# Pre-activation convolution with quantised weights: another mix of combined and plain images, later quotients on ScalarE, twelve image tiles

## The chip, the cores and the metric

The kernel runs on one core of one Trainium2 chip. A core has five engines with queues of their own: TensorE (matrix products, PE in the profile, its weight loads PEld), VectorE (DVE), ScalarE (ACT), GpSimd (POOL) and SyncE (SP), which here only issues transfers. The metric is the device time of one execution in microseconds; a profiled execution also gives a span, from the first to the last recorded instruction.

## What is computed

The input x has 160 images of 128 channels and 32 x 32 pixels. Each image is normalised in 32 groups of 4 channels, then convolved 3 x 3 with one of five sets of weights, and added to x. The weights are quantised in two steps from the range of the whole array U. Image i of the kernel's own order belongs to set n = i // 32.

```python
def conv(x, U):                       # N = 5 sets, K = 3, 128 channels
    s1 = (max(U) - min(U)) / 3.0
    v1 = s1 * floor(U / s1)
    s2 = s1 / 5.0
    v2 = s2 * floor((U - v1) / s2)
    w = (v1 + v2).reshape(128 * N, 128, 3, 3)
    xb = x.reshape(160 // N, N * 128, 32, 32)
    return conv_general_dilated(xb, w, padding=1, feature_group_count=N)

def gn(v, G=32, eps=1e-5):            # per image and group of 4 channels
    return (v - mean) / sqrt(var + eps)

out = x + conv(gn(x), U)
```

## The kernel before

The order of all work is written out by hand: `run` loops over the 160 images, and each engine gets its instructions in the order in which that loop emits them. Images are loaded in pairs into tiles of a pool `xpool` (11 tiles of two images), `LOAD_LEAD` = 18 images ahead. They are measured (sum and sum of squares, on ScalarE but for the eight images of `BY_VECTOR`) `STAT_LEAD` + 1 images ahead. Then the normalised image is split into a 16-bit high and a 16-bit low part, so that products of 16-bit numbers keep enough precision.

The convolution exists in two forms, chosen by `combined(i)`:

- A plain image has z (normalised, 32 bits; GpSimd at L668 or ScalarE at L594), `hi` (ScalarE, L602), `lo` (VectorE, L697) and three combinations of rows of lo (VectorE, L710, L718, L719, tile `rows`). On TensorE the high part goes through nine taps for even and odd rows (18 matmuls, `taps`), the low part through 12 products of combinations (`product`): 30 matmuls.
- A combined image has sums and differences of neighbouring columns of x in a tile `v` of 2048 numbers (GpSimd L632 and L662, VectorE L644 and L651), its high part `vh` (ScalarE, L684) and its low part `vl` (VectorE, L690). Both parts go through 12 products: 24 matmuls.

Before the change images from 7 to 125 are combined when odd, those from 126 (`FIFTHS`) to 145 three in five, and from 146 (`THIRDS`) two in three.

For each image `sums_of_pairs(i + 1)` leaves two partial results in PSUM, ScalarE copies one out (`leave`, L837), VectorE makes the sum and the difference of the two (`pairs`, L846 and L848) as the start of that image's output banks `eo`, and `main` adds the other products to them. The result is added to x in one of two ways (`residual`): ScalarE copies eo to a tile `sum` (L874) and GpSimd issues a transfer that adds it to the image's tile (`accumulate`, L897), or, for images of `by_hand`, VectorE adds it itself (L891). `store` writes a finished pair of images to memory from SP's queue, in which loads, stores and weight loads (`load_set`, L448) stand in one order.

The weights of set n + 1 are made while set n runs. `load_set` fetches them; `make_column` is a generator that makes one column of the 3 x 3 taps; each `take(later, 1)` in the loop emits its next VectorE instruction. The generator's core is `quantise`: a quotient rounded to the nearest integer (`nearest`, L101), five steps that turn it into a floor (L109 to L113), the remainder (L127), and the same again with the second step size. Then the columns are turned by TensorE (`turn_column`), copied to the weight table by ScalarE (L527) and summed by VectorE (`sums_of_set`). The first set is made at the start, where columns alternate between the engines: `over_partitions` brings the range of U to all partitions, `from_range` makes the step sizes, and `warm_up` fills gaps of TensorE with matmuls whose result isn't used.

Of the kernel before, what the change touches and what calls it, by code (L numbers as in the profile page):

```python
# [22 lines left out]
LAST = 4  # L23
# [6 lines left out]

WIDEST = 40.0


class Steps:
# [60 lines left out]

    def nearest(self, pool, v, parts, name, dt, by_scalar=False):

        tag = "m" if by_scalar else "nn"
        n = pool.tile(list(v.shape), dt, tag=tag, name=f"n{tag}_{name}")
        engine = self.nc.scalar.mul if by_scalar else self.nc.vector.tensor_scalar_mul  # L100
        return n, engine(n, v, parts[0])  # L101
# [12 lines left out]

    def quantise(self, pool, un, name, dt, by_scalar=False):


        ints = mybir.dt.int16 if dt == MM else I32
        nn, first = self.nearest(pool, un, self.parts1, name, ints, by_scalar)
# [10 lines left out]
        nn, first = self.nearest(pool, rest, self.parts2, name + "_2", ints)  # L130
        yield first
        yield from self.floor_div(k2, rest, nn, tt, below, self.parts2)
        return k1, k2
# [212 lines left out]
class Main:  # L346
# [24 lines left out]
    STAT_LEAD = 14  # L371
    LOAD_LEAD = 18
    STEADY = 7
    BY_VECTOR = (8, 10, 11, 14, 19, 24, 29, 34)
    FIFTHS = 126
    THIRDS = 146
# [9 lines left out]
    def __init__(self, tc, ctx, keep, x, u, out):  # L386
# [16 lines left out]
        self.upool = pool("u", 1)  # L403
        self.xpool = pool("x", 11)
        self.zpool = pool("z", 3)
        self.parts = pool("parts", 5)
        self.rows = pool("rows", 4)
# [71 lines left out]
    def over_partitions(self, ext1, ident, between):  # L479


        nc, P = self.nc, self.P

        place = self.bank_pair("range").rearrange("p h r w -> p h (r w)")
        rows = place[0:1, 0, : 2 * P].rearrange("p (k c) -> p k c", k=2)
        for k in range(2):
            nc.tensor.transpose(rows[:, k, :], ext1[:, k : k + 1], ident)
        between()
        top = self.const.tile([1, 2], F32, tag="top", name="top")
        nc.vector.tensor_reduce(top, rows, AX.X, ALU.max)  # L490
        spread = place[:, 1, :2]
        nc.tensor.matmul(spread, self.ones, top, start=True, stop=True)
        return spread

    def make_column(self, n, col, by_scalar=False):
# [92 lines left out]

    def normalise(self, i):
        nc = self.nc  # L590
        st = self.stats[self.group_of[i]]
        j = i - self.groups[self.group_of[i]].start
        z = self.zpool.tile([self.P, 1024], F32, tag="z", name=f"z{i}")
        nc.scalar.activation(  # L594
# [10 lines left out]
    def combined(self, i):  # L605
# [142 lines left out]

    def warm_up(self, count):


        zeros = self.los[3].rearrange("p h w -> p (h w)")
        for _ in range(count):
            self.nc.tensor.matmul(
                self.pair[0].rearrange("p i w -> p (i w)"), zeros[:, :128],
                zeros[:, :512], start=True, stop=True,
# [149 lines left out]
    def run(self):  # L906
# [38 lines left out]

        self.ones = self.const.tile([1, P], F32, tag="ones", name="ones")
        nc.vector.memset(self.ones, 1.0)
        ext1 = self.weight_range(list(self.us.values()))
# [16 lines left out]
        def parts(i):  # L965
# [69 lines left out]
        ready, middle, scaled, measured, loaded = [], [], [], self.EARLY, 6  # L1035
        later, turned = iter(()), []
        for i in range(self.imgs):
# [34 lines left out]
            to_measure = range(measured, min(self.imgs, ahead))  # L1072
            measured += len(to_measure)
            if n + 1 < N_SETS:
                if b == (2 if n == 0 else 0):
                    self.load_set(n + 1)
                if b == (4 if n == 0 else 2):
                    later = (s for col in self.COLS for s in self.make_column(n + 1, col))
            by_scalar = [k for k in to_measure if not self.by_vector(k)]
            by_vector = [k for k in to_measure if self.by_vector(k)]  # L1080

            if i < self.FIRST:

# [14 lines left out]
            else:  # L1098
# [8 lines left out]
                last = take(later, 1, last)  # L1107
                for st in scaled:
# [32 lines left out]
            for n_of, col in turned:  # L1141
                self.keep_taps(n_of, col)
                if col == self.COLS[-1]:
                    later = self.sums_of_set(n_of)
            turned = []

            if i >= self.FIRST:
# [5 lines left out]
                else:  # L1153
                    take(later, 1)
                if b == self.per_set - 4:
                    run(later)
                for st in ready:
# [65 lines left out]
```

## Time and profile before

| | us |
|---|---|
| median of 3 runs | 983.02 |
| the three runs | 983.02, 977.3, 989.84 |
| the profiled execution | 982.18 |
| its span | 980.5 |

The page of the profile gives each engine's busy time, share of the span and number of instructions, and the share of a chain of waits that is followed back from the last instruction. A row of a group has the line in the code, the engine, the operation, the tiles written and read with their shapes, how often it occurs, then its busy time in us and the mean of one in ns, then the idle time of the engine just before it and who ended that. A row of a stretch of time has, for each engine, the busy time and the number of instructions, then the clock granted to TensorE, the share of the 16 DMA engines and GB/s. An interval is read with care: successive instructions of one engine overlap a little, so sums of means are somewhat larger than the time they take together.

The transfers, from the page:

| transfer | count | KB each | median us to landing |
|---|---|---|---|
| load of a pair of images (SP) | 78 | 1024 | 7.0 |
| store of a pair (SP) | 78 | 1024 | 8.7 |
| adding a sum to an image (POOL) | 137 | 512 | 7.2 |
| weights of a set (SP) | 4 | 576 | 9.7 |

### The profile page before, as it was taken

The page shows a single profiled execution, that of the slowest core. Times are in us where ns is not written, and L with a number is a line of the kernel's source. Part 1 is how long each engine was busy: PE and PEld are TensorE (multiplying, and loading weights), DVE is VectorE, ACT ScalarE, POOL GpSimd, SP SyncE. Part 2 cuts the span into 40 slices and gives each one's busy share as a digit, 9 for nine tenths or more (in the row PEclk, how much of TensorE's full clock was granted, in tenths as well). Part 3 has the DMA queues.
Part 4 walks back from the last instruction along what each step waited for, and adds up shares of the span by engine and source line. Part 5 has one row for each costly group of instructions (what it writes and reads, how often), then busy time and mean ns, then how long its engine had stood idle before and what let it go on. Part 6 is the DMA issues. An engine that isn't in the chain of part 4 may idle for free.

```text
span 980.5 us, 13236 instructions
## 1 busy us (share of the span) xinstructions
PE 943.3 (96%) x4504; PEld 440.8 (45%) x4504; DVE 913.8 (93%) x1332; ACT 833.4 (85%) x1135; POOL 353.5 (36%) x441
## 2 busy tenths in 40 slices
PE   2899999999999999999999999999999999999997
PEld 1444444444444444444444444444444444444443
DVE  7999999998999999899999998799999998989995
ACT  5779889999999999889898989698989899898551
POOL 4353333343333333333343333233433434333530
PEclk9999999999999999999999999999999999999999
DMA  9627889999998888999998999998989989998774
GB/s 352 264 95 207 230 236 267 265 250 257 319 297 242 269 232 244 257 289 273 250 267 240 272 247 253 285 281 265 239 261 259 258 249 269 247 247 251 178 207 160
DMA packets 65117, 245.86 MB, mean 251 GB/s; under 512 B 5008, under 2 KB 5008, under 8 KB 65040
## 3 DMA queue, kind: packets, MB, share of 16 engines
q1 hardware_dynamic: 45312, 173.09, 49.4%
q0 software_dynamic: 19728, 71.84, 38.8%
q8 instruction: 37, 0.61, 0.2%
q14 instruction: 40, 0.33, 0.1%
HBM read 89.19 MB, written 83.89 MB: 177 GB/s over the span
## 4 chain that ended last, share of the span: by engine, by line
PE 74%; DVE 12%; DMA 6%; issue 4%; ACT 2%; POOL 2%; SPq 0%; DVEq 0%; POOLq 0%
PE eo L789 25%; PE eo L734 23%; PE m L789 12%; PE m1b L789 8%; PE m1a L789 5%; DMA out_dram<-xt 3%; DVE vl L690 2%; DVE v L644 1%; DMA u<-in_L_conv_U_dram 1%; DVE lo L697 1%; DVE eo L846 1%; DMA xt<-sum 1%; DMA range<-in_L_conv_U_dram 1%; DVE eo L848 1%; DVE v L651 1%
## 5 line engine op out<-in xcount | busy, mean ns | idle before, releaser
L734 PE MATMUL eo<-hi,wt 128*128 128x496 f16 (+2 forms) x1386 | 367.7, 375 | 0.7 <-ACT wt L527 0.7
L789 PEld LDWEIGHTS <-wt 128*128 128x128 f16 x1884 | 183.9, 99 | 216.1 <-DVE rows L719 5.2
L734 PEld LDWEIGHTS <-wt 128*128 128x128 f16 x1458 | 142.6, 99 | 163.7 <-ACT wt L527 1.4
L874 ACT COPY sum<-eo 128x1024 f32<-128x1024 f32 x137 | 143.1, 1045 | 63.2 <-PE eo L789 63.0
L690 DVE SCALAR_TENSOR_TENSOR vl<-v,rstd,vh 128x2048 f16<-128x2048 f32 x82 | 192.2, 2344 | 1.4 <-ACT vh L684 1.4
L789 PE MATMUL eo<-vh,wt 128*128 128x496 f16 (+1 forms) x492 | 185.0, 376 | 1.0 <-DVE eo L848 0.9
L789 PE MATMUL eo<-vl,wt 128*128 128x496 f16 (+1 forms) x492 | 184.9, 376 | 0.0
L684 ACT ACTIVATE vh<-v,rstd 128x2048 f16<-128x2048 f32 x82 | 164.1, 2001 | 17.1 <-DVE v L651 16.9
L209 ACT ACTIVATE junk<-xt,mv 128x1024 f16<-128x1024 f32 x152 | 174.3, 1147 | 0.1
L202 ACT ACTIVATE junk<-xt 128x1024 f16<-128x1024 f32 x152 | 160.6, 1057 | 15.2 <-DMA xt<-in_x_dram 11.6
L789 PE MATMUL eo<-rows,wt 128*128 128x496 f16 (+1 forms) x450 | 170.8, 380 | 0.0
L789 PEld LDWEIGHTS <-across 128*128 128x128 f16 x984 | 96.2, 98 | 116.0 <-issue 5.1
L668 POOL TENSOR_SCALAR z<-xt,ngm,rstd 128x1024 f32<-128x1024 f32 x53 | 62.8, 1184 | 232.3 <-DVE tt L109 39.6
L632 POOL TENSOR_SCALAR v<-xt,ngm 128x64 f32<-128x64 f32 x82 | 30.9, 377 | 257.1 <-issue 72.7
L897 POOL DMA_DIRECT2D xt<-sum x137 | 119.8, 878 | 4.4 <-ACT sum L874 3.1
L837 ACT ACTIVATE m<-m 128x512 f32<-128x512 f32 x157 | 94.0, 599 | 24.9 <-PE m L789 18.7
L644 DVE TENSOR_TENSOR v<-xt 128x960 f32<-128x960 f32 x82 | 106.2, 1295 | 2.8 <-POOL v L632 2.8
L789 PE MATMUL m<-vl,across 128*128 128x496 f16 (+1 forms) x246 | 92.1, 374 | 3.3 <-DVE vl L690 3.2
L697 DVE TENSOR_TENSOR lo<-z,hi 128x1024 f16<-128x1024 f32 x78 | 94.9, 1216 | 0.0
L789 PE MATMUL m<-vh,across 128*128 128x496 f16 (+1 forms) x246 | 92.1, 375 | 0.0
L662 POOL TENSOR_TENSOR v<-xt 128x512 f32<-128x512 f32 x82 | 84.8, 1034 | 0.0
L602 ACT CAST hi<-z 128x1024 f16<-128x1024 f32 x78 | 81.5, 1044 | 1.2 <-POOL z L668 0.5
(144 smaller groups left out, 1151.8 us busy)
## 6 DMA issues: line engine op xcount, KB each, us to landing
xt<-in_x_dram SPq DMA_DIRECT2D x78, 1024.0 KB, 7.0
out_dram<-xt SPq DMA_DIRECT2D x78, 1024.0 KB, 8.7
xt<-sum POOLq DMA_DIRECT2D x137, 512.0 KB, 7.2
u<-in_L_conv_U_dram SPq DMA_DIRECT2D x4, 576.0 KB, 9.7
xt<-in_x_dram SPq DMA_DIRECT2D x4, 512.0 KB, 9.9
range<-in_L_conv_U_dram SPq DMA_DIRECT2D x3, 576.0 KB, 8.1
out_dram<-xt SPq DMA_DIRECT2D x3, 512.0 KB, 2.7
u<-in_L_conv_U_dram SPq DMA_DIRECT2D x2, 288.0 KB, 3.0
```

What stands on the lines that cost most here:

```text
L202: self.nc.scalar.activation(junk, image, ACTF.Copy, scale=-1.0 / image.shape[1], accum_out=self.mv[:, j, 0:1],)
L209: self.nc.scalar.activation(junk, image, ACTF.Square, bias=self.mv[:, j, 0:1], accum_out=self.mv[:, j, 1:2],)
L644: nc.vector.tensor_tensor(self.view(v, 1, (511, 2), (half, H), (1, half - 1)), self.view(x, 1, (1, 2), (W, H), (2, half - 1)), self.view(x ...
L662: ins = nc.gpsimd.tensor_sub(self.v[i][:, 1536:], odd, even)
L684: self.nc.scalar.mul(vh, self.v[i], st.rstd[:, j])
L690: yield self.nc.vector.scalar_tensor_tensor(vl, self.v[i], st.rstd[:, j], self.hi[i], ALU.mult, ALU.subtract)
L697: self.nc.vector.tensor_sub(lo[:, 1 : self.H + 1, :].rearrange("p h w -> p (h w)"), self.z.pop(i), self.hi[i].rearrange("p h w -> p (h w)"),)
L734: nc.tensor.matmul(self.bank(target, a)[:, first:end, c0:c1], self.wts[n, col][:, k, :], tile[:, s0 : s0 + 2 * (end - first) - 1 : 2, c0 + ...
L789: self.nc.tensor.matmul(out, weights, moving, start=start and j == 0, stop=False, skip_group_check=True)
L837: self.nc.scalar.mul(m2, self.m2_ps, 0.5)
L874: nc.scalar.copy(self.as_banks(i, self.sum[i]), self.flat(i, eo))
L897: self.nc.gpsimd.dma_start(self.image(i), self.sum.pop(i), accum_op=ALU.add)
```

## The change

It has six parts. `combined` becomes: odd images up to 29, then three in five (i % 5 in 0, 2, 4) up to 145, then three in four. In the weights of sets 1 to 4, both rounded quotients of a column are made by ScalarE: the generator yields a mark `SCALAR` ahead of each, and a new class `Later` passes no further step until `take_scalar`, at the end of the turn, emits it. In the first set's second column ScalarE makes both quotients. `xpool` has 12 tiles and `LOAD_LEAD` is 20; `zpool` goes from 3 to 2, `parts` from 5 to 4, and the tile that takes ScalarE's unread output is uint8. Weights are fetched earlier (for sets 2 to 4 at turn b = 30, the last but one, of the set two before), their making starts one image earlier, and what is left of it is emitted at b = 28 and b = 30. `by_hand` names every sixteenth image where it named every eighth. At the beginning the range is brought to all partitions by two matmuls with a broadcast operand and one VectorE reduction, image 4 is prepared one turn later, and there are eleven more filling matmuls.

```diff
+class Later:
+    def __init__(self, steps=()):
+        self.steps = iter(steps)
+        self.scalar = False
+    def take(self, count, last=None):
+        for _ in range(count):
+            if not self.scalar:
+                step = next(self.steps, None)
+                self.scalar = step is SCALAR
+                last = last if self.scalar else step or last
+        return last
+    def take_scalar(self):
+        if self.scalar:
+            next(self.steps)
+            self.scalar = False
+    def finish(self):
+        run(self.steps)
...
-    def quantise(self, pool, un, name, dt, by_scalar=False):
+    def quantise(self, pool, un, name, dt, by_scalar=()):
...
+        if "later" in by_scalar:
+            yield SCALAR
+        nn, first = self.nearest(
+            pool, un, self.parts1, name, ints, 1 in by_scalar,
+            "m" if 1 in by_scalar and "later" not in by_scalar else "nn",
+        )
...
-    LOAD_LEAD = 18
+    LOAD_LEAD = 20
-    FIFTHS = 126
+    FIFTHS = 30
...
-        self.xpool = pool("x", 11)
-        self.zpool = pool("z", 3)
-        self.parts = pool("parts", 5)
+        self.xpool = pool("x", 12)
+        self.zpool = pool("z", 2)
+        self.parts = pool("parts", 4)
...
-        rows = place[0:1, 0, : 2 * P].rearrange("p (k c) -> p k c", k=2)
+        rows = place[:, 0, : 2 * P].rearrange("p (k c) -> p k c", k=2)
         for k in range(2):
-            nc.tensor.transpose(rows[:, k, :], ext1[:, k : k + 1], ident)
+            nc.tensor.matmul(
+                rows[:, k, :], ext1[:, k : k + 1].to_broadcast([P, P]), ident,
+                start=True, stop=True,
+            )
         between()
-        top = self.const.tile([1, 2], F32, tag="top", name="top")
-        nc.vector.tensor_reduce(top, rows, AX.X, ALU.max)
-        spread = place[:, 1, :2]
-        nc.tensor.matmul(spread, self.ones, top, start=True, stop=True)
+        spread = self.const.tile([P, 2], F32, tag="top", name="top")
+        nc.vector.tensor_reduce(spread, rows, AX.X, ALU.max)
         return spread
...
-            junk = self.unread.tile([self.P, 1024], MM, tag="junk", name=f"junk{i}_{s}")
+            junk = self.unread.tile([self.P, 1024], mybir.dt.uint8, tag="junk", name=f"junk{i}_{s}")
...
+        if i == self.FIRST - 1:
+            z = self.sums.tile([self.P, 1024], F32, tag="sum", name=f"z{i}")
...
-        return (i - self.FIFTHS) % 5 % 2 == 0 if i < self.THIRDS else i % 3 != 1
+        return i % 5 % 2 == 0 if i < self.THIRDS else i % 4 != 2
...
-        if i < self.FIRST or i >= self.imgs - LAST:
-            return True
-        return i > self.BY_VECTOR[-1] - 4 and i % 8 == 7
+        return i < self.FIRST or i >= self.imgs - LAST or i > self.FIFTHS and i % 16 == 7
...
-            self.make_column(0, col, by_scalar=col != self.COLS[0]) for col in self.COLS
+            self.make_column(0, col, by_scalar=which)
+            for col, which in zip(self.COLS, ((), (1, 2), (1,)))
...
         take(third, 1)
+        take(second, 1)
         measure(1, 4)
+        self.warm_up(9, self.m1b)
         run(second)
         self.keep_column(0, self.COLS[1])
+        self.warm_up(2, self.m1b)
...
+            if i == 2:
+                self.load_set(1)
+            if b == self.per_set - 2 and n + 2 < N_SETS:
+                self.load_set(n + 2)
             if n + 1 < N_SETS:
-                if b == (2 if n == 0 else 0):
-                    self.load_set(n + 1)
-                if b == (4 if n == 0 else 2):
-                    later = (s for col in self.COLS for s in self.make_column(n + 1, col))
+                if b == (4 if n == 0 else 1):
+                    later = Later(
+                        s for col in self.COLS for s in self.make_column(n + 1, col, (1, 2, "later"))
+                    )
...
                 if i == 0:
                     measure(0, 8, 9, 10)
+                if i == 1:
                     self.normalise(4)
                     self.high_part(4)
...
-                    take(later, 1)
+                    later.take(1)
+                later.take_scalar()
-                if b == self.per_set - 4:
-                    run(later)
+                if b in (self.per_set - 4, self.per_set - 2):
+                    later.finish()
```

More of the change, by code (lines that the diff above doesn't have):

```diff
@@ L31 @@
 WIDEST = 40.0
+SCALAR = "the next step is ScalarE's"
+class Later:
[15 more added lines that the diff above has]
+        run(self.steps)
 class Steps:
@@ L94, in choose, with nearest @@
         nc.vector.tensor_copy(self.far, far)
-    def nearest(self, pool, v, parts, name, dt, by_scalar=False):
-        tag = "m" if by_scalar else "nn"
+    def nearest(self, pool, v, parts, name, dt, by_scalar=False, tag="nn"):
         n = pool.tile(list(v.shape), dt, tag=tag, name=f"n{tag}_{name}")
@@ L113, in floor_div @@
         yield nc.vector.tensor_sub(k, n, below)
-    def quantise(self, pool, un, name, dt, by_scalar=False):
+    def quantise(self, pool, un, name, dt, by_scalar=()):
         ints = mybir.dt.int16 if dt == MM else I32
-        nn, first = self.nearest(pool, un, self.parts1, name, ints, by_scalar)
+        if "later" in by_scalar:
[4 more added lines that the diff above has]
+        )
         yield first
@@ L129, in quantise @@
         )
-        nn, first = self.nearest(pool, rest, self.parts2, name + "_2", ints)
+        if "later" in by_scalar:
+            yield SCALAR
+        nn, first = self.nearest(
+            pool, rest, self.parts2, name + "_2", ints, 2 in by_scalar
+        )
         yield first
@@ L484, in over_partitions, with make_column @@
         place = self.bank_pair("range").rearrange("p h r w -> p h (r w)")
-        rows = place[0:1, 0, : 2 * P].rearrange("p (k c) -> p k c", k=2)
+        rows = place[:, 0, : 2 * P].rearrange("p (k c) -> p k c", k=2)
         for k in range(2):
-            nc.tensor.transpose(rows[:, k, :], ext1[:, k : k + 1], ident)
+            nc.tensor.matmul(
+                rows[:, k, :], ext1[:, k : k + 1].to_broadcast([P, P]), ident,
+                start=True, stop=True,
+            )
         between()
-        top = self.const.tile([1, 2], F32, tag="top", name="top")
-        nc.vector.tensor_reduce(top, rows, AX.X, ALU.max)
-        spread = place[:, 1, :2]
-        nc.tensor.matmul(spread, self.ones, top, start=True, stop=True)
+        spread = self.const.tile([P, 2], F32, tag="top", name="top")
+        nc.vector.tensor_reduce(spread, rows, AX.X, ALU.max)
         return spread
-    def make_column(self, n, col, by_scalar=False):
+    def make_column(self, n, col, by_scalar=()):
         nc, P = self.nc, self.P
@@ L592, in normalise @@
         j = i - self.groups[self.group_of[i]].start
-        z = self.zpool.tile([self.P, 1024], F32, tag="z", name=f"z{i}")
+        if i == self.FIRST - 1:
+            z = self.sums.tile([self.P, 1024], F32, tag="sum", name=f"z{i}")
+        else:
+            z = self.zpool.tile([self.P, 1024], F32, tag="z", name=f"z{i}")
         nc.scalar.activation(
@@ L747, in bank, with warm_up @@
         return target[h] if target is self.pair else target[:, h]
-    def warm_up(self, count):
+    def warm_up(self, count, bank=None):
         zeros = self.los[3].rearrange("p h w -> p (h w)")
@@ L754, in warm_up @@
             self.nc.tensor.matmul(
-                self.pair[0].rearrange("p i w -> p (i w)"), zeros[:, :128],
+                (bank or self.pair[0]).rearrange("p i w -> p (i w)"), zeros[:, :128],
                 zeros[:, :512], start=True, stop=True,
@@ L944, in run @@
             self.los.append(lo)
-        self.ones = self.const.tile([1, P], F32, tag="ones", name="ones")
-        nc.vector.memset(self.ones, 1.0)
         ext1 = self.weight_range(list(self.us.values()))
@@ L1035, in run @@
         ready, middle, scaled, measured, loaded = [], [], [], self.EARLY, 6
-        later, turned = iter(()), []
+        later, turned = Later(), []
         for i in range(self.imgs):
@@ L1073, in run @@
             measured += len(to_measure)
+            if i == 2:
+                self.load_set(1)
+            if b == self.per_set - 2 and n + 2 < N_SETS:
+                self.load_set(n + 2)
             if n + 1 < N_SETS:
-                if b == (2 if n == 0 else 0):
-                    self.load_set(n + 1)
-                if b == (4 if n == 0 else 2):
-                    later = (s for col in self.COLS for s in self.make_column(n + 1, col))
+                if b == (4 if n == 0 else 1):
+                    later = Later(
+                        s for col in self.COLS for s in self.make_column(n + 1, col, (1, 2, "later"))
+                    )
             by_scalar = [k for k in to_measure if not self.by_vector(k)]
@@ L1104, in run @@
                     self.low_part(i + 2)
-                    take(later, 1)
+                    later.take(1)
                     last = last_of(self.combinations(i + 2))
-                last = take(later, 1, last)
+                last = later.take(1, last)
                 for st in scaled:
@@ L1143, in run @@
                 if col == self.COLS[-1]:
-                    later = self.sums_of_set(n_of)
+                    later = Later(self.sums_of_set(n_of))
             turned = []
@@ L1153, in run @@
                 else:
-                    take(later, 1)
-                if b == self.per_set - 4:
-                    run(later)
+                    later.take(1)
+                later.take_scalar()
+                if b in (self.per_set - 4, self.per_set - 2):
+                    later.finish()
                 for st in ready:
```

## The prediction

> **What bounds the kernel now.** I read the page's busy shares and the shares of its chain of waits first.
>
> ```profile
> PE 943.3 (96%) x4504; PEld 440.8 (45%) x4504; DVE 913.8 (93%) x1332; ACT 833.4 (85%) x1135; POOL 353.5 (36%) x441
> ...
> PE 74%; DVE 12%; DMA 6%; issue 4%; ACT 2%; POOL 2%; SPq 0%; DVEq 0%; POOLq 0%
> ```
>
> TensorE carries the chain, with VectorE close behind. Next, the busy times by stretch of the span (engines in the order PE, PEld, DVE, ACT, POOL; at the end the clock, the DMA share and GB/s).
>
> ```profile
> 175.00:200.00 25.00, 24.43 (x118) 11.31 (x117) 24.79 (x36) 23.45 (x32) 8.76 (x13) 1.00 0.93 263
> 300.00:350.00 50.00, 50.00 (x242) 23.45 (x241) 49.47 (x76) 44.72 (x63) 17.93 (x21) 1.00 0.86 246
> 600.00:650.00 50.00, 47.80 (x221) 21.59 (x220) 41.05 (x58) 41.80 (x58) 15.28 (x18) 0.97 0.93 268
> 800.00:850.00 50.00, 50.00 (x240) 23.31 (x238) 45.37 (x57) 46.52 (x64) 18.94 (x22) 1.00 0.97 266
> ```
>
> TensorE is full from 200 us on but for one stretch. VectorE is full (99%) where later weights are being made (300 to 350) and has a tenth free where they are not (800 to 850, already three combined images in five). Before 200 us it is VectorE that is full, and TensorE loses 4.3 us between 100 and 200 (95.7 us busy). Third, the groups by shape give prices.
>
> ```profile
> L690 DVE SCALAR_TENSOR_TENSOR vl<-v,rstd,vh 128x2048 f16<-128x2048 f32 x82 | 192.2, 2344 | 1.4 <-ACT vh L684 1.4
> L684 ACT ACTIVATE vh<-v,rstd 128x2048 f16<-128x2048 f32 x82 | 164.1, 2001 | 17.1 <-DVE v L651 16.9
> L644 DVE TENSOR_TENSOR v<-xt 128x960 f32<-128x960 f32 x82 | 106.2, 1295 | 2.8 <-POOL v L632 2.8
> L697 DVE TENSOR_TENSOR lo<-z,hi 128x1024 f16<-128x1024 f32 x78 | 94.9, 1216 | 0.0
> L602 ACT CAST hi<-z 128x1024 f16<-128x1024 f32 x78 | 81.5, 1044 | 1.2 <-POOL z L668 0.5
> L651 DVE SCALAR_TENSOR_TENSOR v<-xt,twice 128x512 f32<-128x512 f32 x82 | 60.7, 741 | 0.0
> L710 DVE TENSOR_TENSOR rows<-lo 128x1024 f16<-128x1024 f16 x75 | 51.3, 684 | 0.8
> L718 DVE TENSOR_TENSOR rows<-lo 128x512 f16<-128x512 f16 x75 | 31.1, 415 | 0.0
> L719 DVE TENSOR_TENSOR rows<-lo 128x512 f16<-128x512 f16 x75 | 31.1, 414 | 0.0
> L101 DVE TENSOR_SCALAR nnn<-u,s1r 128x384 int16<-128x384 f32 x13 | 6.2, 477 | 6.1 <-DMA u<-in_L_conv_U_dram 6.0
> L101 DVE TENSOR_SCALAR nnn<-rest,s2r 128x384 int16<-128x384 f32 x15 | 6.2, 414 | 0.0
> L101 ACT ACTIVATE nm<-u,s1r 128x384 int16<-128x384 f32 x2 | 1.6, 806 | 0.1
> ```
>
> A combined image costs VectorE 1295 + 741 + 2344 = 4380 ns, a plain one 1216 + 684 + 415 + 414 = 2729 ns; ScalarE 2001 against 1044. One wait stands out in VectorE's own list, and the timeline shows it:
>
> ```profile
> 614.19 0.46 SPq L448 DMA_DIRECT2D u<-in_L_conv_U_dram  x1
> ...
> 626.17 0.47 DVE L101 TENSOR_SCALAR nnn<-u,s1r 128x384 int16<-128x384 f32 x1 [5.95 <-DMA u<-in_L_conv_U_dram]
> ...
> 627.98 0.82 PE L789 MATMUL m<-rows,wt 128*128 128x512 f16 x3 [2.01 <-DVE rows L719]
> ```
>
> The weights' transfer was issued late and took 12 us; VectorE stood 5.95 us in front of its first step, the rows of the next image came late, TensorE stood 2.0 us and then ran some matmuls at 0.6 us. From the starts of the second combination (L848), images 29 to 61 take 185.2 us, 61 to 93 185.2, 93 to 125 (with this wait) 190.95: it cost 5.7 us.
>
> **What the skill says.** The page "TensorE: Matmul & The Clock Gate" (section "Wait — 56ns, not 53.3ns?") gives N/2.4 GHz plus 2.5 ns per warm matmul, an estimate of 1.268 us for one of 512 and two of 496 columns, twice; the chain shows 1.27 for six, so TensorE has no slack inside and only fewer matmuls help. "ScalarE: Activation LUTs" ("What ACT_TABLE_LOAD costs") gives 186 + 0.833 N ns plus 93 for a pointer operand: 599 ns for N = 384, as an estimate; the trace has 806 for the strided weights (that value is used) and nothing for the contiguous remainder (I take 0.6). "Trainium Kernel Development and Optimization" ("Key Constraints") says that all queues run on the same 16 DMA engines; the trace agrees: 49.4% and 38.8% of the engines for the two queues, and 0.86 to 1.00 together in the stretches.
>
> **The change, part by part.**
>
> TensorE. A combined image has 24 matmuls, a plain one 30. Counting combined() over the images: 82 before, 92 after (12 and 12 below image 30; 48 and 58 from 30 to 125; 12 and 12 to 145; 10 and 10 in the last 14). 10 x 6 x 1.27/6 = **-12.7 us**, on the path. Check: images 125 to 157 (21 of 32 combined) took 178.1 us against 185.2 with 16, that is 1.4 each, weights' transposes included.
>
> VectorE. +10 x 1.651 = +16.5; 24 quotients of later weights leave, 12 x 0.477 + 12 x 0.414 = -10.7; additions by hand fall from 16 to 8, 8 x 1.217 (L891) = -9.7; one early quotient -0.4. Net -4.3. But the work sits in images 32 to 127: per five images, start to start in the timeline (combined 5.50, plain 3.74, pairs included), 3 x 5.50 + 2 x 3.74 + 0.9 (statistics, by hand) = 24.9, and some 7 weight steps of 0.48 = 3.3: 28.2 us. TensorE: 3 x 5.08 + 2 x 6.35 + 0.3 = 28.2. Before, the same count in the weight stretches is 46.7 against 46.3 per eight images, and eight images took 46.9 to 47.1 there, 45.0 between. So this balance was a little worse before and was caught up in the gaps; now the gaps are shorter (the steps spread to image 28 or so of a set).
>
> ScalarE. +10 x 0.957 = 9.6; quotients 12 x 0.806 + 12 x 0.6 + 0.6 = 17.5; 8 more sum copies x 1.045 = 8.4; plain group starts fall by 7, x 1.239 (L594) = -8.7. Net +26.8: from 91% to some 97% in the middle. Covered by its waiting for eo (29 us between 200 and 550 us in its list of waits), which shrinks to about a third. Queued behind each quotient on ScalarE is the next image's sum copy; who waits for a late quotient is VectorE.
>
> GpSimd. +10 x (0.377 + 1.034) - 3 x 1.184 + 8 x 0.878 = +17.5, of 353: hidden by 64% idle.
>
> DMA. Eight more accumulating transfers: 38.8% of 980.5 over 137 is 2.78 us of all engines each, +22 us, so 0.95 in the middle becomes about 0.99. Per image 2 x 0.524 + 15/16 x 0.524 + 0.02 = 1.56 MB; the stretches' GB/s over share give 265 to 300 GB/s, mean 278: 5.60 us, against TensorE's 5.64. Twelve tiles and a lead of 20 give two images (11 us) more to absorb it. Each load on SP still waits for the store before last of its tile, and stores for their sums (568 and 243 us of SP's waits): not altered.
>
> The late weights. The load moves from the first image of a set to two images earlier, its first use from the third image to the end of the second: about 8 us more lead against a wait of 5.95. I take **-5.0** (0 to -5.7). On SP it stands before that image's store; the old weights were read by then, so SP does not stop for it.
>
> First set. Six quotients (2.7 us) leave VectorE and the steps stretch over 26 images instead of 22: of TensorE's 4.3 us I take **-2.5** (0 to -4.3).
>
> Beginning. One reduction over all partitions replaces reduction, matmul and read-back (17.89 to 18.97 us): -0.7; the second column's quotient -0.45 on the way to 40.01 us; nine filling matmuls of 0.21 last 1.9 us in a gap of 1.87 that is now about a half shorter: +0.4. Together **-0.7** (-1.5 to +0.5). Fewer z and hi buffers: the third z moves to the sums' pool and image 4 moves one turn later, when hi of image 0 has been read (by 52.5 us; hi of 4 came at 54.9): nothing, at worst six of its matmuls, 1.3 us. uint8 junk: nothing that a row shows, 0 either way. End mix: VectorE 3 x 5.50 + 3.74 = 20.2 per four images against 21.6: 0, +-1.5.
>
> Friction. Nothing in the trace runs three engines and DMA at 97 to 99% together. Bound: 0, or all that DMA at its worst rate takes (14, below). I take **+3**.
>
> Sum: 982.2 (span 980.5 and 1.7 around it) - 12.7 - 5.0 - 2.5 - 0.7 + 3 = **964.3**. The median, 983.0, is 0.8 us from that execution, so I predict 964.
>
> **Rivals.**
> Transfers bind: at 265 GB/s an image needs 5.88 us, 0.24 over, x 110 images = 26, less 11 of lead and the 3 counted: +12, 976. For: share 1.00 in one stretch. Against: 300 GB/s in that same one.
> All gains whole, no friction: 982.2 - 12.7 - 5.7 - 4.3 - 1.5 = 958. For: three in five already ran without a TensorE gap after 800 us. Against: no weights were made there.
> Slower: VectorE waits for ScalarE's quotients. It is in order, so the low part, the rows and the pairs of the next image stand behind it, and TensorE behind them. VectorE now starts on vl about 3 us after vh is done, and the quotient comes some 2.2 us after vh; if ScalarE's lag eats that margin, 24 quotients (L109's wait) each cost up to 2 us: 964 + 45 = 1009. It passes 983 from 0.8 us per quotient. Against: ScalarE still has 3%.
> That the change does not do what it says: matmul counts would stay at 4504; the two sets of numbers in combined() exclude it.
>
> **Numbers.** Forecast 0.58 (956 to 973, half of it below 963.4), 958 0.11, transfers 0.22, slower 0.09 (0.07 beyond 2%). With 2% (what can be told from no change) at 963.4 and 1002.7: faster 0.40, same 0.53, slower 0.07. The range 954 to 983 leaves out the slower case and tails of the fast one.
>
> **What would show it.** TensorE busy near 933 with about 4455 matmuls; no wait for u at L101; a TensorE-full stretch at 28.2 us per five images; ScalarE at 97% in the middle; load waits not growing. Wrong if VectorE shows waits at L109, if ScalarE waits for xt in the middle, or if TensorE has gaps in images 32 to 127.

## The result, and the profile after

The changed kernel takes 989.62 us (median of 22 runs, 985.08 to 1007.4), the kernel before in the same session 982.87 (22 runs, 977.3 to 995.59): ratio 1.0081, 95% interval 1.0052 to 1.0111. It was forecast 19 us faster and is some 7 to 8 slower. A ratio here leaves out executions that lie more than about 1.5% above their kernel's fastest; where the executions of an experiment spread, their median and extremes are given too, and the argument goes by stretches of the profiled execution.

Busy times and shares of the chain of waits, of the page after:

```profile
PE 936.4 (95%) x4455; PEld 436.6 (44%) x4455; DVE 918.0 (93%) x1288; ACT 854.9 (87%) x1161; POOL 373.2 (38%) x466
...
PE 44%; DVE 35%; issue 9%; ACT 8%; POOL 2%; DMA 0%; DVEq 0%; POOLq 0%; ACTq 0%
```

The matmuls fell by 49, to the number forecast (60 fewer in the images, 11 more filling ones). But TensorE's share of the chain went from 74% to 44% and VectorE's from 12% to 35%: what ends the program now passes through VectorE again and again. The busy times by stretch (columns as before):

```profile
300.00:350.00 50.00, 49.70 (x240) 23.32 (x239) 49.01 (x72) 48.22 (x68) 19.50 (x23) 1.00 1.00 274
...
600.00:650.00 50.00, 50.00 (x240) 23.37 (x239) 48.29 (x70) 48.01 (x68) 20.73 (x25) 1.00 1.00 262
...
700.00:750.00 50.00, 47.35 (x228) 22.03 (x226) 47.68 (x65) 45.01 (x62) 19.82 (x24) 1.00 0.96 265
...
800.00:850.00 50.00, 50.00 (x240) 23.38 (x239) 43.71 (x57) 48.14 (x67) 20.03 (x25) 1.00 0.99 275
```

The gap at 600 to 650 of before (47.80, the late weights' transfer) is closed. In its place TensorE loses a little in many stretches where weights are made (700 to 750: 2.65 us), and nothing at 800 to 850, where none are made. The list of waits names the places (who waited, for what: us in total, times, longest), of the kernel after. In it `m` is one of the two partial results of `sums_of_pairs`, and also ScalarE's copy of it; `across` holds sums of a set's weights over their columns:

```profile
PE m L828 <- DVE vl L729: 14.8, 15, 2.1
PE m L828 <- DVE across L568: 3.7, 1, 3.7
...
DVE v L683 <- POOL v L671: 8.5, 11, 0.9
...
DVE tt L135 <- ACT nnn L127: 0.9, 1, 0.9
```

TensorE's new idle time is mostly 15 short waits for the low parts `vl`, 1 us each in the mean, and one wait for the sums of set 1's weights. VectorE's waits for ScalarE's quotients are 0.9 us in all. The starts of the second combination (L848 before, L887 after) in the timeline cut the span into pieces. (The prediction numbers these images one too low: its "29 to 61" is 30 to 62, and so on; its last stretch then holds 20 combined images of 32, not 21.) The other rows are the experiments below, each from its profiled execution.

| us | to 30 | 30 to 62 | 62 to 94 | 94 to 126 | 126 to the end |
|---|---|---|---|---|---|
| before | 223.3 | 185.2 | 185.2 | 190.9 (u late) | 195.8 |
| after | 222.5 | 190.8 | 187.0 | 188.3 | 197.9 |
| hand8 | 222.3 | 191.5 | 185.5 | 190.4 | 197.6 |
| quot_vec | 225.8 | 186.3 | 186.8 | 189.0 | 199.1 |
| finish25 | 225.5 | 184.8 | 187.0 | 188.2 | 197.7 |
| before_nw | 218.2 | 184.7 | 184.7 | 185.8 | 196.4 |
| after_nw | 218.9 | 180.6 | 179.3 | 189.0 | 206.0 |
| after_nw_hand8 | 218.5 | 180.5 | 180.4 | 192.2 | 204.9 |
| mix_old_hand8 | 219.9 | 185.4 | 185.2 | 186.3 | 196.4 |

A boundary that moves by one image can shift a piece by some 4 us (after, 61 to 93: 191.2 instead of 187.0), so a small difference of single pieces says little.

Eleven of the twelve waits for `vl` from 260 to 790 us are at one place: TensorE wants `m` of the image whose number is 4 modulo 5. One of them in the timeline (start, duration, engine, line):

```profile
377.23 1.21 DVE L736 TENSOR_TENSOR lo<-z,hi 128x1024 f16<-128x1024 f32 x1
378.37 0.60 DVE L136 SCALAR_TENSOR_TENSOR tt<-nnn,s2nlo,tt 128x384 f32<-128x384 int16 x1
...
380.17 0.60 DVE L137 SCALAR_TENSOR_TENSOR tt<-tt,s2r,nnn 128x384 f32<-128x384 f32 x1
380.70 1.21 DVE L928 TENSOR_TENSOR xt<-eo,xt 128x1024 f32<-128x1024 f32 x1
382.05 0.70 DVE L885 SCALAR_TENSOR_TENSOR eo<-m1b,m 128x512 f32<-128x512 f32 x1
...
383.39 1.15 DVE L683 TENSOR_TENSOR v<-xt 128x960 f32<-128x960 f32 x1
...
385.12 2.35 DVE L729 SCALAR_TENSOR_TENSOR vl<-v,rstd,vh 128x2048 f16<-128x2048 f32 x1
...
387.52 0.38 PE L828 MATMUL m<-vl,across 128*128 128x512 f16 x1 [0.76 <-DVE vl L729]
```

VectorE works here without a gap: the low part and the rows of image 58, two weight steps, an addition by hand (which comes only every sixteenth image), the pairs of image 57 and the combination of image 60, then `vl` of image 59. TensorE has come through the short combined image 57 by then and waits for it.

### The profile page after: what moved, and what is told of

The parts are those of the page before. It is cut to its first block, busy times and chain, and to the rows that moved or that the text cites. A ratio compares the mean times of both kernels' runs of the same rounds, so it can differ in the third digit from the quotient of the medians.

```text
span 986.4 us, 13160 instructions
## 1 busy us (share of the span) xinstructions
PE 936.4 (95%) x4455; PEld 436.6 (44%) x4455; DVE 918.0 (93%) x1288; ACT 854.9 (87%) x1161; POOL 373.2 (38%) x466
## 4 chain that ended last, share of the span: by engine, by line
PE 44%; DVE 35%; issue 9%; ACT 8%; POOL 2%; DMA 0%; DVEq 0%; POOLq 0%; ACTq 0%
PE eo L773 14%; PE eo L828 12%; PE m L828 8%; DVE v L683 6%; DVE vl L729 6%; PE m1b L828 4%; DVE eo L885 4%; PE m1a L828 4%; DVE lo L736 3%; DVE v L690 3%; DVE eo L887 3%; ACT vh L723 2%; ACT junk L244 2%; POOL rstd L282 2%; DVE rows L757 1%
## 5 line engine op out<-in xcount | busy, mean ns | idle before, releaser
L773 PE MATMUL eo<-hi,wt 128*128 128x496 f16 (+3 forms) x1206 | 320.3, 376 | 1.2 <-DVE eo L887 0.7
L828 PEld LDWEIGHTS <-wt 128*128 128x128 f16 x1884 | 183.2, 99 | 213.2 <-DVE rows L758 4.7
L729 DVE SCALAR_TENSOR_TENSOR vl<-v,rstd,vh 128x2048 f16<-128x2048 f32 x92 | 215.6, 2343 | 0.5 <-ACT vh L723 0.5
L828 PE MATMUL eo<-vh,wt 128*128 128x512 f16 x552 | 206.8, 375 | 0.3 <-DVE eo L887 0.3
L828 PE MATMUL eo<-vl,wt 128*128 128x512 f16 x552 | 206.7, 375 | 0.0
L723 ACT ACTIVATE vh<-v,rstd 128x2048 f16<-128x2048 f32 x92 | 184.0, 2000 | 22.0 <-DVE v L690 12.2
L773 PEld LDWEIGHTS <-wt 128*128 128x128 f16 x1278 | 125.1, 99 | 146.1 <-DVE eo L887 1.8
L244 ACT ACTIVATE junk<-xt,mv 128x1024 uint8<-128x1024 f32 x152 | 174.2, 1146 | 0.1
L237 ACT ACTIVATE junk<-xt 128x1024 uint8<-128x1024 f32 x152 | 160.3, 1055 | 12.4 <-DMA xt<-in_x_dram 9.4
L828 PE MATMUL eo<-rows,wt 128*128 128x496 f16 (+1 forms) x390 | 148.1, 380 | 0.0
L683 DVE TENSOR_TENSOR v<-xt 128x960 f32<-128x960 f32 x92 | 124.0, 1348 | 8.5 <-POOL v L671 8.5
L701 POOL TENSOR_TENSOR v<-xt 128x512 f32<-128x512 f32 x92 | 94.9, 1032 | 0.0
```

Source lines behind the costliest of these rows:

```text
L237: self.nc.scalar.activation(junk, image, ACTF.Copy, scale=-1.0 / image.shape[1], accum_out=self.mv[:, j, 0:1],)
L244: self.nc.scalar.activation(junk, image, ACTF.Square, bias=self.mv[:, j, 0:1], accum_out=self.mv[:, j, 1:2],)
L683: nc.vector.tensor_tensor(self.view(v, 1, (511, 2), (half, H), (1, half - 1)), self.view(x, 1, (1, 2), (W, H), (2, half - 1)), self.view(x ...
L701: ins = nc.gpsimd.tensor_sub(self.v[i][:, 1536:], odd, even)
L723: self.nc.scalar.mul(vh, self.v[i], st.rstd[:, j])
L729: yield self.nc.vector.scalar_tensor_tensor(vl, self.v[i], st.rstd[:, j], self.hi[i], ALU.mult, ALU.subtract)
```

## The experiments

All were compared with the kernel before on the same chip (its medians 981.74, 982.6, 979.71 and 982.21 us in the four sessions).

**Parts of the load moved (mix_old, quot_vec, hand8, finish25).** Three theories stood at first: VectorE's pace (V), ScalarE's (S), the transfers (D).

```diff
mix_old, in combined():
-        if i < self.FIFTHS:
+        if i < 126:
-        return i % 5 % 2 == 0 if i < self.THIRDS else i % 4 != 2
+        return (i - 126) % 5 % 2 == 0 if i < self.THIRDS else i % 3 != 1
quot_vec:
-  self.make_column(n + 1, col, (1, 2, "later"))
+  self.make_column(n + 1, col)
hand8, in by_hand():
-  i > self.FIFTHS and i % 16 == 7
+  i > self.FIFTHS and i % 8 == 7
finish25:
-  if b in (self.per_set - 4, self.per_set - 2):
+  if b in (self.per_set - 7, self.per_set - 4, self.per_set - 2) and (n == 0 or b > self.per_set - 7):
```

> The changed kernel with the mix of before (odd images to 125, three in five to 145, two in three after), all else as changed. Theory V (VectorE sets the pace of images 32 to 127 with its own work and the waits it has between in-order neighbours, so the extra combined images cost it more than they save TensorE): VectorE gets back 16.5 us, TensorE is the bound again, the wait for the weights' transfer is gone: 975 to 980. Rival S (ScalarE's later quotients and eight more sum copies hold the others up): 985 to 990, as changed. Rival D (the DMA engines are full): 985 to 990, since the transfers are the same.

> The changed kernel with the 24 later quotients on VectorE again. Theory V: 10.7 us more on the engine that sets the pace: 996 to 1000. Rival S: the quotients were what VectorE and the sum copies waited for: 980 to 985. Rival D: 989, unchanged.

> The changed kernel with every eighth image added by VectorE, as before. Theory V: 9.7 us more on VectorE: 995 to 999. Rival S: 8.4 us less on ScalarE: 981 to 985. Rival D: 22 us less of the DMA engines' time: 975 to 983.

> The changed kernel with what is left of the columns of set 1 emitted at image 25 of set 0 instead of 28. TensorE stood 3.7 us before image 32 for the sums of its weights, and eight images there took 51.5 us against 45 to 48. If that is the weights' late end: 983 to 986. If VectorE is merely late in general there: 989, unchanged, or a little more by the burst.

quot_vec took 989.55 us (988.8 to 991.25; ratio 1.008, 1.0046 to 1.0114), hand8 989.46 (988.2 to 990.72; 1.0087, 1.0058 to 1.0117). With 24 quotients back on VectorE, or eight more additions by it, nothing changes in the total; nor does it help that ScalarE or the transfers have less. So no plain sum of one engine's work explains the loss: each of the three simple theories missed at least once (D's "unchanged" held for quot_vec, and its gain failed to come in hand8). finish25 took 986.35 (982.32 to 1004.13; 1.0042, 1.0012 to 1.0073), just above its expected 983 to 986: the piece after image 30 went from 190.8 to 184.8 us, and the one up to it grew by 3.0, since the same steps are done earlier. The late weights of set 1 are one cause, worth some 3 us. The wait for these sums is gone in quot_vec too, where no step has to pause for ScalarE; so against finish25 its additional work on VectorE does cost some 3 us.

mix_old spread: 975.11 once, 992.41 to 1000.89 in the five others. The profiled execution is one of the five (992.41), and its list of waits has:

```profile
ACT nnn L127 <- DMA u<-in_L_conv_U_dram: 21.3, 2, 11.1
...
DVE tt L135 <- ACT nnn L127: 18.5, 2, 9.7
...
PE m L828 <- ACT m L876: 12.0, 2, 6.5
```

The first quotient of a set stands on ScalarE until `u` has landed, and everything of ScalarE's stands behind it. That the execution of 975 is one without that stall is not shown by any trace; but it is the first sign that the new mix is what costs, and mix_old_hand8 below confirms it.

**Group starts (before_even, mix8, mix8_vec, mix8_fin).** The statistics come in groups of eight images. Before, the first image of each group from 24 on to 120 was plain; with `i % 5` eight of those from 32 to 120 are combined. The timeline of the kernel after at one of them (image 80; TensorE waits for the low part of image 79, which VectorE makes after the combination of image 80):

```profile
499.85 1.66 POOL L282 TENSOR_TENSOR rstd<-ve,mhalf 128x8 f32<-128x8 f32 x1 [4.48 <-DVE tt L137]
...
501.51 0.37 POOL L671 TENSOR_SCALAR v<-xt,ngm 128x64 f32<-128x64 f32 x1
501.85 1.03 POOL L701 TENSOR_TENSOR v<-xt 128x512 f32<-128x512 f32 x1
501.92 1.98 DVE L683 TENSOR_TENSOR v<-xt 128x960 f32<-128x960 f32 x1 [0.88 <-POOL v L671]
...
504.82 2.34 DVE L729 SCALAR_TENSOR_TENSOR vl<-v,rstd,vh 128x2048 f16<-128x2048 f32 x1
...
507.22 0.38 PE L828 MATMUL m<-vl,across 128*128 128x512 f16 x1 [2.08 <-DVE vl L729]
```

GpSimd's power for `rstd` stands ahead of its outer columns; VectorE waits 0.88 us for these, then its subtraction runs beside GpSimd's and takes 1.98 us, where the one at 383.39 above took 1.15; TensorE loses 2.08. The Trainium skill's page "GPSIMD Engine Reference" (section "1. Specifications") says that GpSimd's SBUF interfaces are shared with VectorE, in contention when VectorE reads two SBUF inputs. This subtraction reads two; the trace agrees, with 1.98 us beside GpSimd's subtraction of L701 and 1.15 at 383.39, where GpSimd was idle. Of the 92 in the kernel after, eleven take 1.9 us or more (5 of 82 before, 17 in before_even).

```diff
before_even (the kernel before):
-            return i % 2 == 1
+            return i % 2 == (i < 30)
mix8 (the changed kernel):
-        return i % 5 % 2 == 0 if i < self.THIRDS else i % 4 != 2
+        return i % 8 in (1, 3, 4, 6, 7) if i < self.THIRDS else i % 4 != 2
mix8_vec: mix8 and quot_vec;  mix8_fin: mix8 and finish25
```

> The kernel before, with the even images from 30 on combined instead of the odd ones (to image 125; as many, 48). All twelve group starts from 32 to 120 are then combined, and nothing else is changed: same work on every engine. Theory G: twelve starts by 1.5 to 2 us of TensorE's waiting, 998 to 1007 us, with the waits of TensorE for vl of some 2 us at each. Rival (which image starts a group does not matter): 980 to 986 us.

> The changed kernel with the combined images of 30 to 145 chosen by i % 8 in (1, 3, 4, 6, 7) instead of i % 5 in (0, 2, 4): five of eight (73 instead of 70 combined), but no image that starts a statistics group of eight is combined any more. Theory G (group starts): where a group's first image is combined, GpSimd's outer columns stand behind its own power for rstd, VectorE's combination and the scales behind them, and TensorE waits some 2 us for the low parts; with that gone and 18 more matmuls (3.8 us) saved, 968 to 975 us. Rival (the images combined cost VectorE and ScalarE what they save TensorE, wherever they stand): 987 to 992 us. Shown by: the waits of TensorE for vl of about 2 us (15 of them, 14.8 us in the changed kernel) are nearly gone with G, and stay with the rival.

> The five-of-eight mix with plain group starts, and the later weights' 24 quotients on VectorE again. If ScalarE's waiting for the weights' transfer at the first quotient costs something, or ScalarE binds, this is faster than the five-of-eight mix alone by 2 to 10 us; if VectorE binds once the starts are plain (some 20 us more work on it), slower by 5 to 15 us; Theory G alone: within 3 us of it, 968 to 976.

> The five-of-eight mix with plain group starts, and the columns of the second set of weights finished at image 25 instead of 28. Late weights and group starts as two separate costs: 3 us less than the five-of-eight mix alone, 964 to 972 us. If one was the other's shadow: the same as the five-of-eight mix.

before_even took 989.17 us (985.6 to 998.04; ratio 1.0069, 1.0034 to 1.0105). A group start that is combined costs (989.17 - 982.6) / 12 = 0.55 us, real but a third of what was expected. Its expectation is wrong in calling the work on every engine the same: the z of the twelve starts moves from ScalarE (L594, 25 times before and 13 now, 1.24 us each) to GpSimd (L668, 53 and 65), so 0.55 is what is left with ScalarE relieved. TensorE's waits in it after 215 us are not for `vl` (0.5 us) but for rows (4.1) and for the pairs (5.7). In the rows by shape of before_even, VectorE's subtraction shows it (busy, mean ns of one, then the idle time ahead of it; before: 106.2, 1295 and 2.8):

```profile
L644 DVE TENSOR_TENSOR v<-xt 128x960 f32<-128x960 f32 x82 | 114.0, 1390 | 10.9 <-POOL v L632 10.9
```

mix8, where no group start up to image 145 is combined, took 993.98 (982.73 to 1004.82; ratio 1.0081, 1.0051 to 1.011), mix8_vec 999.51 (986.47 to 1005.72; 1.0138, 1.0108 to 1.0169), mix8_fin 998.05 (994.22 to 1008.67; 1.0178, 1.012 to 1.0236, six runs). None of the gains expected of the three came. Theory G as the main cause falls: VectorE's wait for GpSimd is down from 8.5 to 1.4 us in mix8, and the waits of TensorE for `vl` are still there, somewhat shorter (13.6 us in all, as many as 18; 16.6 in mix8_vec, 13.7 in mix8_fin). What came on top, in mix8's list of waits (its profiled execution is the longest of the 22, 1004.82; the two others have such waits too):

```profile
ACT junk L237 <- DMA xt<-in_x_dram: 35.0, 17, 7.9
...
ACT nnn L127 <- DMA u<-in_L_conv_U_dram: 16.1, 2, 9.3
...
PE m L828 <- DVE vl L729: 13.6, 18, 1.5
...
DVE v L683 <- POOL v L671: 1.4, 3, 0.9
```

ScalarE waits for images and weights to land. In the kernel after it did so for 9.4 us, all early in the program.

**Room on VectorE, and the transfers behind it (after_nw, before_nw, even_vec, mix_old_early).** "nw" leaves out the work on the later weights: all five sets are computed with the weights of set 0.

```diff
after_nw, before_nw: in taps() and product()
-        n, _ = self.place(i)
+        n = 0
and in run() the making of later columns is taken out:
-                    later = Later(s for col in self.COLS for s in self.make_column(n + 1, col, ...))
even_vec (on quot_vec):
-                    later.take(1)
+                    if not self.combined(i + 4):
+                        later.take(1)
...
-                    later.take(1)
+                    later.take(2 if self.combined(i + 2) else 1)
mix_old_early (on mix_old):
-            if b == self.per_set - 2 and n + 2 < N_SETS:
+            if b == self.per_set - (2 if n == 0 else 6) and n + 2 < N_SETS:
```

> The changed kernel without the later weights' work: sets 1 to 4 are computed with the weights of set 0, so that VectorE's 42 steps a set, ScalarE's six quotients and three copies, and TensorE's nine transposes a set are left out (the u transfers stay). Theory R (in the weights' stretches VectorE has no room, so that the low parts of the image at place 4 of each five come late): TensorE's 14.8 us of waits for vl and the 3.7 us for late sums go, and 36 transposes, 960 to 968 us, TensorE at 50.0 in the windows of 50 us. Rival (the mix itself, by ScalarE, GpSimd or the transfers, sets the pace): 978 us or more.

> The kernel before without the later weights' work, left out in the same way (set 0's weights for all sets). Its TensorE was at 50.0 of 50 in nearly every window, so only the transposes and the late u go: 973 to 979 us. Theory R: the changed kernel without the weights is then 9 to 15 us faster than this one, which is what the mix saves TensorE. Rival: the two are within 4 us.

> The changed kernel with the quotients on VectorE (as in the run quot_vec), and one weight step moved out of every iteration that has both a plain image's low part and a combination, to the end of the next iteration that has a combined image's low part and no combination. If the waits for vl come from bunching only, they go to under 5 us and the time to 975 to 981 us; if VectorE has no room at all in the weights' stretches (Theory R without bunching), 986 to 991 us as in quot_vec.

> The changed kernel with the old mix of combined images (as in the run mix_old), and the u transfers of sets 3 and 4 issued four images earlier (place 26 of the set instead of 30; the columns are done by 25). Theory U (ScalarE stands still at the first quotient until u has landed, some 10 us each in sets 2 and 3): both stalls go in every execution, 972 to 978 us, faster than the kernel before by 5 to 10 us. Rival (the stalls have another cause, or another transfer is late instead): 985 us or more, with ScalarE's waits for u or DVE's for an x tile still there.

before_nw took 971.38 us (970.23 to 984.62; ratio 0.993, 0.9889 to 0.997), a little better than expected. after_nw is split. In its first two sets the mix pays all that it should: 180.6 and 179.3 us against 184.7 and 184.7 of before_nw, 4.1 and 5.4 us for three more combined images each (1.27 each: 3.8; with the ends one image earlier it is 3.6 and 3.8). The group starts are combined in these sets too and cost nothing: with room on VectorE they are absorbed. TensorE is full; from 600 us on it no longer is:

```profile
300.00:350.00 50.00, 50.00 (x240) 23.36 (x239) 42.82 (x58) 48.58 (x64) 19.76 (x23) 1.00 1.00 258
...
550.00:600.00 50.00, 50.00 (x240) 23.37 (x239) 44.57 (x59) 46.72 (x64) 18.36 (x22) 1.00 0.97 256
600.00:650.00 50.00, 45.97 (x219) 21.20 (x217) 38.85 (x50) 41.10 (x57) 17.81 (x20) 1.00 0.96 262
```

The list of waits of after_nw after 240 us gives the reason:

```profile
ACT junk L237 <- DMA xt<-in_x_dram: 35.0, 20, 3.5
```

Images come late to ScalarE's statistics, which hold up its `m`, for which TensorE waits. Over its 22 runs that is 960.74 to 993.23 us, median 981.97, 10.6 more than before_nw, where 9 to 15 less was expected (the ratio, 0.9835, 0.9764 to 0.9907, rests on 960.74 and 969.96 alone; the profiled execution took 975.55). So Theory R was right in the first half and its rival in the second: with room on VectorE, and with the smaller pools in place, the mix works, and then the images come late.

even_vec took 990.92 (990.24 to 993.66; ratio 1.0116, 1.006 to 1.0173), with 18.0 us of waits for `vl`: moving one step in five images to a lighter turn doesn't help (four runs). Other orders were not tried. mix_old_early took 993.85 (974.6 to 1004.7, two of 14 below 976; 1.0017, 0.9966 to 1.0067): in its profiled execution (994.18) the waits for `u` are gone, and 46.7 us of waits for images after 240 us stand in their place (8.1 in mix_old). Theory U was right in what holds ScalarE and wrong in what removing it gains. That the earlier transfer pushes the others back fits, but is not shown by itself.

**What the transfers fall behind (after_nw_hand8, mix_old_hand8, before_hand16).** The change moved eight residuals from VectorE to accumulating transfers. These runs put them back, or move them alone:

```diff
after_nw_hand8, mix_old_hand8 (the latter on mix_old_early): as in hand8
before_hand16 (the kernel before):
-        return i > self.BY_VECTOR[-1] - 4 and i % 8 == 7
+        return i > self.BY_VECTOR[-1] - 4 and i % 16 == 7
```

> The changed kernel without the later weights' work (sets 1 to 4 with set 0's weights, as in the run after_nw) and with the residual of every eighth image added by VectorE again instead of every sixteenth, so that eight accumulating transfers of 512 KB less go through GpSimd's queue, as in the kernel before. Theory D (once VectorE has room, the transfers are what the pace falls behind: ScalarE waits for x tiles and TensorE for ScalarE): 958 to 964 us, closely together, ScalarE's waits for x after 240 us under 5 us instead of 35, every set about 180 us. Rival (the drift of the run without weights has another cause): 975 to 985 us with a spread of 20 us, as there.

> The changed kernel with the old mix, the early u transfers (as in the run mix_old_early) and the residual of every eighth image by VectorE. What is left of the change is the new beginning and first set, the tiles, the quotients on ScalarE and the new end mix. Theory D: the waits for x that made that run 975 to 1005 us go; 970 to 977 us, closely together, which beats both kernels. Rival: spread and median stay at 985 to 994 us.

> The kernel before with one part of the change alone: every sixteenth residual by VectorE instead of every eighth; eight more accumulating transfers of 512 KB (4.2 MB more on 245.9), 9.7 us less on VectorE. Theory D: executions spread from 978 to 1000 us, median 986 to 994, with waits of ScalarE for x tiles and of VectorE for u. Rival (VectorE's room is all that counts): 972 to 981 us, closely together.

after_nw_hand8 took 975.64 us (963.43 to 985.79; ratio 0.9902, 0.9869 to 0.9935), 6 less than after_nw, but it drifts in the same way, to 192.2 us in the third set. So the eight transfers are a part, and the larger part is left: with the eight transfers or without them, the DMA engines move some 260 GB/s there (249 to 280 in the windows from 650 to 900 us of both). The lag begins earlier: from 200 to 600 us the windows of after_nw move 266 GB/s in the mean, where 32 images of 1.56 MB in 180 us would be 277, an estimate. Whether the engines' rate is the limit or the order on SP's queue isn't shown. The DMA engines' share in the drifting windows of after_nw_hand8 is 0.91 to 0.99, and SP stands in front of loads for 554 of the 720 us from 240 to 960 until an older store has landed (370 us in the kernel after, 405 in mix_old_hand8). No run changes that order alone. before_hand16 took 985.59 (977.81 to 999.77; 1.0022, 0.9993 to 1.0051): its executions spread as Theory D said, but those of the kernel before do so too (976.91 to 999.5 there), the median lies just below the expected range and the ratio doesn't separate it from no change.

mix_old_hand8 took 975.27 us (973.68 to 995.98, 16 of 22 below 976.4; ratio 0.9948, 0.9921 to 0.9975). It beats both kernels. Its expectation names the new end mix among what is left; that was an error, the end mix too was the old one here. TensorE is full in its windows, VectorE at 89 to 97%, and the share of the transfers below 1:

```profile
250.00:300.00 50.00, 50.00 (x241) 23.42 (x240) 48.72 (x74) 46.03 (x66) 17.70 (x21) 1.00 0.96 274
...
600.00:650.00 50.00, 50.00 (x240) 23.33 (x239) 46.60 (x68) 46.55 (x65) 18.65 (x22) 1.00 0.91 255
```

Its list has no wait for `u` or for an image after 240 us. hand8 differs from it in the mixes and in when `u` of sets 3 and 4 is issued, and takes 989.46. Since hand8's list has no wait for `u` after the beginning either, the new mixes are what costs some 14 us; the rest of the change, without the moved residuals and with the earlier `u`, gains 7 by the medians and 2 to 8 by the ratio's interval.

## Why the prediction was wrong

**TensorE's -12.7** is right as a price: 4455 matmuls as counted, and some 4 to 5 us a set where nothing else binds (after_nw against before_nw). Its own check of 1.4 us an image is 1.8 with the 20 combined images that its stretch really holds. Busy time fell only to 936.4 instead of 933: after two of the waits, of 3.7 and 2.1 us, 14 matmuls followed each other at some 0.42 us instead of 0.21 (clock 0.97 in two windows of 50 us).

**"Friction. I take +3"** is the step that failed. It stood for all that happens when VectorE and TensorE need 28.2 us each for five images; the bound put beside it was 14 (15 by its own sum, 26 - 11), and only for transfers. From image 30 to 126 the terms without it give 561.4 - 12.7 - 5.0 = 543.7 us; measured were 566.0, so it was 22. Of these TensorE's idle time is 17.4 (it was busy for 548.6 of the 566.0): 11.4 for `vl`, 3.7 for the late sums of set 1, 2.3 for rows and pairs. The slowed matmuls make about 3 more (14 by 0.21); the rest, some 2, isn't placed. With what the first set (2.4) and the end mix (2.1) missed, the 19.3 that friction was short make up the way from 964.3 to the 988.1 of the profiled execution.

The equality itself was the warning: VectorE takes its work in a fixed order, tied to TensorE by the pairs, and catches up only where it has room. The old mix left it the stretches between (the prediction's own 45.0 us for eight images there, against 46.9 to 47.1 where weights are made); the new one spread the steps over those. From image 30 to 126 VectorE was busy for 539.5 us, all but 4 of the 543.7 that the forecast's terms leave for TensorE; in mix_old_hand8 it was 526.6 of 556.9, with TensorE full. That the room is what is missing is shown by leaving the weights out (479.7 us busy in that stretch; this takes ScalarE's quotients out too, but quot_vec shows that these alone don't matter). More work on VectorE costs less than it adds: some 3 us in quot_vec against finish25, and nothing in hand8, where VectorE's idle time in that stretch falls from 26.6 to 20.3 us instead. Why it can use this idle time for additions and not for an earlier `vl` stays open.

**"Late weights -5.0"** held: the wait for `u` is gone in the profiled execution. But two things were missed. A set's steps now end only at the turns b = 28 and 30, and set 1's sums were late (finish25: 3 us). And where `u` is late, the first quotient stops ScalarE (21.3 us in mix_old) instead of VectorE (6.0 before).

**Group starts** weren't counted at all: which images are combined, not only how many. Eight of them by 0.55 us of before_even are about 4 us, an estimate, inside the 22.

**First set -2.5 and beginning -0.7**: 0.8 us gained up to image 30 in the profiled execution, -3.5 with the old mix from image 30 on (mix_old 219.8, mix_old_hand8 219.9). So the gain exists, and the new mix reaches back into it. **End mix "0, +-1.5"**: +2.1; TensorE waits 1.53 and 0.87 us for `vl` at 924 and 947 us, and 1.53 and 0.88 at the same two images in after_nw, so here the weights are not the cause.

**VectorE's -4.3** is +4.2; 4.9 of the difference is its subtraction, 1348 ns instead of 1295 in the mean, 92 times. **ScalarE, GpSimd, DMA**: +21.5 instead of +26.8, +19.7 for 17.5, and the accumulating queue from 380 to 401 us of all engines, +21 for 22. ScalarE's 97% didn't come, since TensorE never ran at the pace that would need it. The quotients took 811 and 601 ns, as priced.

**The rivals.** VectorE waiting for ScalarE's quotients (1009) is excluded: 0.9 us in all. Transfers binding at 976: not in the kernel after, but next in line. Its pace was right and the forecast's too high: sets that drift take 189.0 us for 32 images of 1.56 MB (after_nw) and 192.2 for 1.53 MB (after_nw_hand8), 264 and 254 GB/s, and not the 278 that were taken as the mean; what holds the transfers to it stays open. Had VectorE had room, 964 would still not have been reached as a median: after_nw, with that work left out altogether, has 982, and after_nw_hand8 976.

## What to carry to other kernels

When the sums of two engines come out equal over a period, that is no balance to bank on: here it cost 22 us, more than the 17.7 that were to be gained there. Price such a tie at the loss of the gain, and look where the slower engine has been catching up until now. Beside how many items of a periodic schedule change kind, list which ones, against every other period in the program (here statistics groups of 8, sets of 32, additions by hand every 16). And before moving work off the bound engine, work out from bytes and the lowest sustained GB/s of a long stretch what the transfers have done so far and what the new pace asks of them: in after_nw twelve tiles hid their lag for two sets of five and then no longer.

## What was not expected of the hardware

VectorE's subtraction of 128x960 takes 1.15 us where nothing of GpSimd's subtraction of 128x512 falls into it, about 1.31 where 0.3 us of that do, and 1.98 where 0.97 do, 0.83 longer. A pause of TensorE of 2.08 us (before 507.22) was followed by eight matmuls at about half their rate, one of 2.09 us (before 741.76) by none. One program ran in 960.74 and in 993.23 us (after_nw) where images came late, while before_nw held ten of twelve runs within 2.4 us. Weights of 576 KB landed in a median of 7.1 us in the kernel after, and in 13.6 in mix8, at about the same mean rate (253 and 249 GB/s).
